# Weight quantisation in single steps, totals ahead of shares, and two input tiles moved, in a four-layer kernel

## The chip, the cores and the metric

The kernel runs on one core of one Trainium2 chip. A core has five engines that each work through their own queue of instructions in order: TensorE (PE in the profile, with its weight loads as PEld), VectorE (DVE), ScalarE (ACT), GpSimd (POOL) and SyncE (SP), which here issues DMAs. They wait for one another by semaphores. Matrix products are accumulated in PSUM banks of 128 partitions by 512 fp32 numbers; everything else lives in SBUF. The metric is the device time of one execution in microseconds (us), smaller is better.

## The reference

x has 2 sequences of 1024 tokens with 512 features. Four residual layers follow each other:

```python
x = x + attn_a(layernorm(x), w_in, w_out)                 # linear attention
x = x + ffn(layernorm(x), w_gate_up, w_proj)
x = x + attn_b(layernorm(x), Wq1, Wq2, Wk, Wv, Wlam, Wo)  # softmax attention
x = x + ffn(layernorm(x), w_gate_up, w_proj)              # same weights again
```

Linear attention projects to q, k, v, a and g. With k = tanh(k), a = clip(sigmoid(a + 2), 0.6, 0.9995) and u = k·v it runs a recurrence along the tokens, mem = a·mem + u, in chunks of 64, and returns (gate·(q·mem) + (1 − gate)·v) @ w_out.T, with q scaled by its root mean square per head and gate = sigmoid(g).

The feed-forward first makes its weights ternary: in groups of 64 numbers, scale = mean(|w|), and w becomes −scale, 0 or +scale, whichever of round(w / scale) it is. Then silu(x @ Wg)·(x @ Wu), an RMS norm, and the product with the ternary w_proj.

Attention b is differential: 16 heads, two sets of queries, causal softmax for each, and

```python
y = softmax(q1 k^T / sqrt(d)) v - sigmoid(x Wlam) * softmax(q2 k^T / sqrt(d)) v
```

followed by Wo.

## The kernel before

**Data.** The 2048 tokens lie in 16 residual tiles `xres` of 128 tokens by 512 features. A *block* is 512 tokens, four tiles; there are four blocks t. Features are handled in four *feature chunks* c of 128.

**Stage a, linear attention (14 to 390 us).** For each block, and in it for each feature chunk c: TensorE projects k and v (`kv`) and a and g (`ag`, both L315); ScalarE takes the tanh, the copy of v and the two sigmoids out of PSUM (L446 to L452); GpSimd multiplies u = k·v (L455) and later u·prefix (L466); VectorE clips a, makes the running product `prefix`, scales q (L471), and runs the recurrence as one scan (L477); then mem·q on VectorE (L482), mem − v on GpSimd (L483), mem·gate on VectorE (L484) and the addition of v to `yt` on GpSimd (L485). In the last step (t=3, c=3) the GpSimd work is given to VectorE. When all four `yt` are there, TensorE makes `a_out` (L509) and VectorE adds it to `xres` (L514).

Between these the next block's input is prepared. Its tiles are normalised on VectorE (L128: `xn_a`, one in c=0, one in c=1, two in c=2) and turned (transposed) by TensorE (L137) in c=2 and c=3. In the last block it is the first feed-forward block's input instead: `layernorm_begin` after c=0 (mean and variance on VectorE, L109/L110, and a square root on ScalarE), its reciprocal and four normalised tiles after c=1, the turns in c=3 (`xnt_f`).

**The weights on the side.** The feed-forward weights are quantised during stage a, in 16 *weight chunks* f, each of three tiles of 128 by 512 (class `Ternary`, L178). `begin` takes magnitude and sign on ScalarE, `mean` makes one matmul for each of the three tiles (`pm`, L203), whose result ScalarE casts to `scale`, and `finish` is six VectorE operations on 128x1536 numbers: the maximum with a floor (L208), the comparison `one` (L211), subtract, add, multiply (L213 to L215) and the product with the sign (L216). The result is stored to DRAM (`w_kept`) and the next chunk begins. `quantise(i)` (L361) calls `mean` for i = 0, 1, 2, and for i = 3 the whole finish. The lists `pieces` (L415 to L418) say which of these happen where in a step c.

**What sets the order.** In stage a the orders of TensorE and VectorE are those in which the code calls them (`manual_schedule`), and operations with no such place, the mean and variance of later blocks, are fitted in by a scheduler. The orders of ScalarE and GpSimd come from the scheduler. A tile pool that has no free buffer delays the operation that asks for one.

**Feed-forward 0 (395 to 764 us)** and **feed-forward 1 (1770 us to the end)** go block by block through the 16 weight chunks (L595 the gate and up products, L616 the down product). During one block the next block's input is made: its mean and variance (`layernorm_stats`), four normalised tiles, their turns, ScalarE's cast to `xs` and VectorE's `rest` (L165). The pool of the mean and variance is `norm`, with two buffers of each kind.

**Stage b, attention b (764 to 1770 us).** It goes through 32 pairs of heads, 16 to a sequence, each in `STEPS` = 6 steps. TensorE makes scores `s` (L872), whose maxima VectorE takes (L882, L887), then scores again transposed (`t`, L933, L941), ScalarE the exponential (L949), TensorE the weighted values `y` (L971). `weigh` copies a finished y to `ys` (L988) and sends it on by four DMAs from SyncE: for each of two heads its *share* of the output (L991) and the row of the softmax *totals* (L996, `tot`). When a sequence is done, `divide` (L1001) takes the reciprocal of the totals (48x512, L1004), multiplies the second set by lambda (L1006) and splits the factors in two (L1010, L1011); `combine` (L1013) spreads them by a matmul `r` (L1018), multiplies the shares (L1021) and subtracts them on GpSimd (L1022). `b_out` (L1035) follows. `at(n, step, ...)` hangs such work on a step of a pair. For sequence 0 it lies in the first pairs of sequence 1; for sequence 1 in a tail with its own fixed order on VectorE as well (L1158 to L1184), together with the turns of feed-forward 1's first input (`first_input`, L1047).

Of the kernel before, what the change touches and what calls it, by code (L numbers as in the profile page):

```python
# [14 lines left out]
ALU = mybir.AluOpType  # L15
# [27 lines left out]
def kernel(  # L43
# [59 lines left out]
    def layernorm_begin(tiles, name):  # L103
# [15 lines left out]
    def layernorm_stats(tiles, name):  # L119

        return layernorm_end(*layernorm_begin(tiles, name))
# [56 lines left out]
    class Ternary:  # L178
# [27 lines left out]
        def finish(self, dst):  # L206
            scale, mag = self.scale, self.mag
            nc.vector.tensor_scalar(scale, scale, SCALE_MIN, None, ALU.max)  # L208

            one = self.pool.tile(self.shape, BF, tag="one", name=f"one{self.n}", bufs=1)  # L210
            nc.vector.scalar_tensor_tensor(one, scale, TERNARY_CUT, mag, ALU.mult, ALU.is_lt)  # L211

            nc.vector.tensor_sub(scale, scale, mag)  # L213
            nc.vector.tensor_add(scale, scale, mag)
            nc.vector.tensor_mul(scale, scale, one)  # L215
            nc.vector.tensor_mul(dst, scale, self.sign)  # L216


    with ExitStack() as s:
# [141 lines left out]
        def quantise(i):  # L361

            now = chunk[0]
            if i < 3:
                now.mean(i, bank)
                return
            now.finish(now.w)
            nc.sync.dma_start(out=w_kept[now.f].bitcast(F32), in_=now.w.bitcast(F32))
            chunk.pop(0)
            if chunk:  # L370
                chunk[0].begin()
            if now.f + 3 < NF:
                chunk.append(Ternary(tp, now.f + 3, range(3)))
# [34 lines left out]
        for t in range(NBLK):  # L408
            yt = wa.tile([P, NKC, BLK], F32, tag="yt", name=f"yt{t}")
            last = t == NBLK - 1  # L410
            for c in range(NKC):
# [3 lines left out]
                if not last:  # L415
                    pieces = ((2,), (), (3,)) if c % 2 else ((0,), (1,), ())
                else:
                    pieces = (((0, 1), (2,), (3,)), ((0, 1), (2,), ()), ((), (), ()))[max(c - 1, 0)]  # L418
# [5 lines left out]
                if t + c == 0:  # L424
                    quantise(3)
                if not last and c > 1:
# [16 lines left out]
                if last and c == NKC - 1:  # L443
                    quantise(3)
# [29 lines left out]


# [7 lines left out]
                other.tensor_sub(mem, mem, v)  # L483
                nc.vector.tensor_mul(mem, mem, gate)  # L484
                other.tensor_add(yt[:, c, :], mem, v)  # L485
                if last and c == 0:
# [8 lines left out]
                for i in pieces[2]:  # L495
                    quantise(i)
# [9 lines left out]
            for j, k in products:  # L506
# [5 lines left out]
                if k == NKC - 1:  # L512
                    xi = xres[t * TPB + j]
                    nc.vector.tensor_add(xi, xi, po[j])  # L514
                    if not last:
# [4 lines left out]
                        for i in ((), (), (3, 0), (1, 2, 3))[j]:  # L520
                            quantise(i)
            if not last:
# [725 lines left out]
```

## Time and profile before

| | |
|---|---|
| median of three runs | 2144.16 us (2143.34 to 2144.2) |
| the profiled execution | 2142.4 us, its span 2140.7 us |
| mean granted TensorE clock | 0.994 |
| TensorE busy | 2106.4 us, 98% of the span |
| VectorE busy | 1077.7 us, 50% |
| ScalarE busy | 835.1 us, 39% |
| GpSimd busy | 445.0 us, 21% |

The profile is of one execution. Busy times do not add up to the span, since the engines work beside each other. The windows view splits it by stage; columns are the stretch in us, its length, busy time (and count) of TensorE, its weight loads, VectorE, ScalarE and GpSimd, the mean granted clock, the DMA share and GB/s:

```profile
14.00:104.00 90.00, 90.00 (x235) 42.06 (x234) 55.99 (x70) 38.95 (x56) 22.15 (x16) 1.00 0.34 129
104.00:180.00 76.00, 75.83 (x196) 34.71 (x194) 55.61 (x66) 34.68 (x47) 17.04 (x12) 1.00 0.23 83
180.00:262.00 82.00, 81.76 (x204) 36.85 (x204) 61.53 (x72) 37.13 (x49) 18.60 (x14) 1.00 0.18 67
262.00:390.00 128.00, 115.25 (x286) 52.28 (x285) 99.87 (x134) 47.52 (x68) 24.89 (x19) 0.95 0.22 82
1250.00:1270.00 20.00, 17.43 (x84) 8.23 (x85) 12.89 (x33) 4.64 (x13) 5.46 (x16) 0.83 0.03 8
1720.00:1770.00 50.00, 46.65 (x191) 21.40 (x192) 31.05 (x45) 12.61 (x28) 13.21 (x16) 1.00 0.33 119
```

In a timeline row the first number is the start in us from the beginning of the span, the second how long the instruction (or the group of equal ones, xN) took, then engine, line, operation, output and inputs; in brackets the idle time of the engine before it and what ended that.

### The profile page before, as it was taken

The numbers are of one execution on the slowest core, as the hardware profiler recorded it, in microseconds if no ns is written. First come the engines' busy times: TensorE is split into PE (matmuls) and PEld (weight loads), VectorE is DVE, ScalarE is ACT, GpSimd is POOL, SyncE is SP. The second block draws the span as 40 slices with busy tenths as digits, with TensorE's granted clock in tenths as the row PEclk, the third lists the DMA queues.
The fourth block names the chain that finished last, engine by engine and source line by source line (L and its number), as shares of the span: only waits on it lengthen the run. The fifth ranks groups of instructions, "written<-read, shape, count | busy, mean of one in ns | idle before, by whom it ended". The sixth has DMA issues, their size and how long they took to land.

```text
span 2140.7 us, 28058 instructions
## 1 busy us (share of the span) xinstructions
PE 2106.4 (98%) x10632; PEld 1245.6 (58%) x10632; DVE 1077.7 (50%) x2276; ACT 835.1 (39%) x1589; POOL 445.0 (21%) x808
## 2 busy tenths in 40 slices
PE   8999998899999999999999999999999999999998
PEld 4444444688888854444444444444444447888887
DVE  5676868433434235555555555464646662433332
ACT  5343543244334322444444422343434523333332
POOL 1312212121221221111111113021212221222212
PEclk9999999999999999999999999999999999999999
DMA  7121211600000111111110101201010033000000
GB/s 268 37 83 59 89 71 47 250 1 1 1 1 1 35 47 38 41 26 41 26 41 21 46 8 37 57 19 46 20 33 14 14 111 133 20 1 20 1 21 20
DMA packets 50999, 98.71 MB, mean 46 GB/s; under 512 B 10800, under 2 KB 19120, under 8 KB 50864
## 3 DMA queue, kind: packets, MB, share of 16 engines
q1 hardware_dynamic: 50864, 96.93, 13.8%
q8 instruction: 83, 1.36, 0.3%
q14 instruction: 52, 0.43, 0.1%
HBM read 58.75 MB, written 16.78 MB: 35 GB/s over the span
## 4 chain that ended last, share of the span: by engine, by line
PE 91%; DVE 5%; ACT 1%; issue 1%; POOL 1%; DMA 1%; SPq 0%; DVEq 0%; ACTq 0%; POOLq 0%
PE y L971 13%; PE g L595 11%; PE u L595 11%; PE f_out L616 11%; PE s L872 10%; PE pq L804 8%; PE t L933 8%; PE ag L315 4%; PE kv L315 4%; PE pv L769 3%; PE b_out L1035 2%; PE a_out L509 2%; PE mt L912 1%; PE t L941 1%; DVE one L211 1%
## 5 line engine op out<-in xcount | busy, mean ns | idle before, releaser
L949 ACT ACTIVATE pr<-t 128x512 f32<-128x512 f32 (+3 forms) x768 | 314.7, 497 | 383.5 <-PE t L941 383.3
L882 DVE CUSTOM_DVE_ANT_0 s<-s,causal 128x128 f32<-128x128 f32 (+3 forms) x512 | 245.3, 510 | 126.7 <-PE s L872 117.9
L971 PE MATMUL y<-pr,val 128*64 128x512 f32 (+3 forms) x1536 | 291.6, 501 | 1.3 <-ACT ys L988 1.3
L610 POOL TENSOR_TENSOR ssq<-ssq,sq 128x512 f32<-128x512 f32 x120 | 156.0, 1300 | 606.7 <-ACT sq L609 606.7
L601 DVE TENSOR_TENSOR h<-h,u 128x512 f32<-128x512 f32 x128 | 88.0, 688 | 360.6 <-PE u L595 354.5
L595 PE MATMUL g<-xs,w 128*128 128x512 f32 x1024 | 260.9, 397 | 0.0
L616 PE MATMUL f_out<-w,hs 128*128 128x512 f32 x1024 | 257.7, 394 | 0.3 <-DVE hs L604 0.3
L887 DVE TENSOR_REDUCE nmax<-s 128x1 f32<-128x512 f32 x256 | 164.9, 686 | 181.7 <-PE s L872 181.6
L595 PE MATMUL u<-xs,w 128*128 128x512 f32 x1024 | 256.3, 392 | 0.0
L872 PE MATMUL s<-gr,gr 32*128 32x512 f32 (+3 forms) x1536 | 249.8, 493 | 2.6 <-DVE nmax L882 2.6
L595 PEld LDWEIGHTS u<-xs,w 128*128 128x128 f32 x1024 | 192.2, 188 | 43.4
L616 PEld LDWEIGHTS f_out<-w,hs 128*128 128x128 f32 x1024 | 191.6, 188 | 43.9 <-DVE hs L604 1.1
L595 PEld LDWEIGHTS g<-xs,w 128*128 128x128 f32 x1024 | 190.1, 188 | 42.8 <-issue 1.0
L971 PEld LDWEIGHTS y<-pr,val 128*64 128x64 f32 x1536 | 93.7, 136 | 181.1 <-issue 105.7
L933 PE MATMUL t<-gr,gr 32*128 32x512 f32 (+3 forms) x1536 | 198.8, 533 | 0.0
L804 PE MATMUL pq<-b_xt,w_qk 128*128 128x512 f32 x384 | 176.1, 603 | 0.2 <-DVE x L633 0.2
L872 PEld LDWEIGHTS s<-gr,gr 32*128 32x128 f32 x1536 | 148.6, 186 | 46.7 <-issue 13.3
L603 ACT CAST hs<-h 128x512 fp32r<-128x512 f32 x128 | 79.4, 621 | 236.6 <-DVE h L601 236.6
L600 ACT ACTIVATE h<-g 128x512 f32<-128x512 f32 x128 | 76.6, 598 | 243.6 <-PE g L595 243.5
L952 POOL TENSOR_SCALAR_AFFINE_SELECT pr<-pr 128x256 f32<-128x256 f32 x256 | 101.5, 409 | 331.8 <-ACT pr L949 331.8
L604 DVE TENSOR_TENSOR hs<-h,hs 128x512 fp32r<-128x512 f32 x128 | 88.6, 692 | 83.1 <-ACT hs L603 83.1
L804 PEld LDWEIGHTS pq<-b_xt,w_qk 128*128 128x128 f32 x384 | 69.6, 189 | 88.4 <-issue 74.0
(160 smaller groups left out, 2218.9 us busy)
## 6 DMA issues: line engine op xcount, KB each, us to landing
w<-w_kept SPq DMA_DIRECT2D x32, 768.0 KB, 9.2
w_kept<-w SPq DMA_DIRECT2D x16, 768.0 KB, 3.2
gr<-gr SPq DMA_DIRECT2D x96, 128.0 KB, 2.3
w<-in_w_gu_dram SPq DMA_DIRECT2D x32, 256.0 KB, 2.9
share<-ys SPq DMA_DIRECT2D x128, 64.0 KB, 2.0
x<-in_x_dram SPq DMA_DIRECT2D x16, 256.0 KB, 6.1
w<-in_w_pt_dram SPq DMA_DIRECT2D x16, 256.0 KB, 3.6
w_qk<-in_wq_dram SPq DMA_DIRECT2D x8, 512.0 KB, 4.5
```

The costliest lines, as they stand in the source:

```text
L315: nc.tensor.matmul(po, w[:, k, ts(c, P)], xt[:, k, :], start=(k == 0), stop=(k == NKC - 1))
L595: nc.tensor.matmul(po, ws[f][:, part, ts(k, P)], xs[:, e, k, :], start=(k == 0 and e == 0), stop=(k == NKC - 1 and e == 1),)
L610: nc.gpsimd.tensor_add(ssq, ssq, sq)
L616: nc.tensor.matmul(po[j], hp[:, e, ts(j, P)], ws[f][:, 2, :], start=(f == 0 and e == 0), stop=(f == NF - 1 and e == 1),)
L804: nc.tensor.matmul(po, w[:, k, ts(kind, P)], xts[b][:, k, ts(e, BLK)], start=(k == 0), stop=(k == NKC - 1),)
L872: nc.tensor.matmul(part, queries[:, ts(j, P)], keys[:, first : first + nk], start=True, stop=True,)
L882: nc.vector.tensor_tensor_reduce(part, part, causal[:, BLK - part.shape[-1] :], -1.0, 3.0e38, ALU.add, ALU.min, top,)
L887: nc.vector.tensor_reduce(top, part, AX.X, ALU.max, negate=True)
L933: nc.tensor.matmul(banks[u, e][:, :nq], keys[:, ts(kb, P)], queries[:, (qb + 1) * BLK - nq : (qb + 1) * BLK], start=True, stop=False,)
L949: nc.scalar.activation(pr[:, e, :nq], banks[u, e][:, :nq], AF.Exp)
L952: nc.gpsimd.affine_select(out=pr[:, :, :P], in_=pr[:, :, :P], compare_op=ALU.is_ge, fill=0.0, base=0, pattern=[[0, 2], [1, P]], channel_mu ...
L971: nc.tensor.matmul(y[64 * e : 64 * e + 64, lo:], all_values[:, HV * (NH * kb + h) : HV * (NH * kb + h) + 64], pr[:, e, : BLK - lo], start= ...
```

## The change

1. `finish` becomes a generator of its six operations, and `quantise(3)` only puts them into a list `steps`. `step(1)` issues one, `step()` all that are left, then the store and the next chunk's `begin`. In the recurrence of a feature chunk, the floor is issued ahead of the scan, the comparison between mem·q and mem·gate, and the other four after mem·gate; the addition to `yt` is called before them.
2. Weight chunks are spread otherwise. Block 0 finishes six (one more: chunk 1 in c=0, 2 in c=1, 3 in c=3), the last block two, chunk 14 in c=0 and 15 in c=1 (before: chunk 13 behind c=0, 14 behind c=1, and 15 in c=3, behind the rests of the feed-forward's input). The three `pm` matmuls move with it. The next layer's `layernorm_begin` is called behind chunk 14's last steps.
3. The mean and variance of the later feed-forward blocks take their buffers from the stage's own pool `fp`, not from `norm`. As the instructions stand in order, those of blocks 1 and 2 of feed-forward 0 (eight pairs of operations) now lie inside the last recurrence, t=3, c=3, and the four of block 1 of feed-forward 1 in the tail of stage b. The square root of the first feed-forward block's variance stands on ScalarE between the two sigmoids of t=3, c=1.
4. `weigh` issues the two rows of totals ahead of the two shares.
5. The reciprocal of `divide` goes in four pieces of 48x128 for sequence 0, with score maxima between them.
6. The turns, casts and rests of the first two input tiles of feed-forward 1 go from the tail into steps 0 and 2 of the last pair, and the order of the tail is combine, turn 2, combine, turn 3, rest 2, rest 3.

```diff
--- before.py
+++ after.py
@@ -100,7 +100,7 @@
 
     norm = ctx.enter_context(tc.tile_pool(name="norm", bufs=2, reuse_waits="tile"))
 
-    def layernorm_begin(tiles, name):
+    def layernorm_begin(tiles, name, norm=norm):
 
         n = len(tiles)
         mv = norm.tile([P, n, 2], F32, tag="ln_mv", name=f"mv_{name}")
@@ -116,9 +116,9 @@
         nc.vector.reciprocal(rstd, rstd)
         return mv, rstd
 
-    def layernorm_stats(tiles, name):
-
-        return layernorm_end(*layernorm_begin(tiles, name))
+    def layernorm_stats(tiles, name, norm=norm):
+
+        return layernorm_end(*layernorm_begin(tiles, name, norm))
 
     def normal(i, j, stats, name, xn=None):
 
@@ -204,16 +204,18 @@
             nc.scalar.copy(self.scale[:, i, :], pm)
 
         def finish(self, dst):
+
             scale, mag = self.scale, self.mag
-            nc.vector.tensor_scalar(scale, scale, SCALE_MIN, None, ALU.max)
+            v = nc.vector
+            yield v.tensor_scalar(scale, scale, SCALE_MIN, None, ALU.max)
 
             one = self.pool.tile(self.shape, BF, tag="one", name=f"one{self.n}", bufs=1)
-            nc.vector.scalar_tensor_tensor(one, scale, TERNARY_CUT, mag, ALU.mult, ALU.is_lt)
-
-            nc.vector.tensor_sub(scale, scale, mag)
-            nc.vector.tensor_add(scale, scale, mag)
-            nc.vector.tensor_mul(scale, scale, one)
-            nc.vector.tensor_mul(dst, scale, self.sign)
+            yield v.scalar_tensor_tensor(one, scale, TERNARY_CUT, mag, ALU.mult, ALU.is_lt)
+
+            yield v.tensor_sub(scale, scale, mag)
+            yield v.tensor_add(scale, scale, mag)
+            yield v.tensor_mul(scale, scale, one)
+            yield v.tensor_mul(dst, scale, self.sign)
 
 
     with ExitStack() as s:
@@ -364,13 +366,24 @@
             if i < 3:
                 now.mean(i, bank)
                 return
-            now.finish(now.w)
-            nc.sync.dma_start(out=w_kept[now.f].bitcast(F32), in_=now.w.bitcast(F32))
-            chunk.pop(0)
-            if chunk:
-                chunk[0].begin()
-            if now.f + 3 < NF:
-                chunk.append(Ternary(tp, now.f + 3, range(3)))
+            steps.extend([now.finish(now.w)] * 6)
+            steps.append(now)
+
+        steps = []
+
+        def step(n=7):
+
+            for _ in range(min(n, len(steps) - 1) if n < 7 else len(steps)):
+                one = steps.pop(0)
+                if one is not chunk[0]:
+                    next(one)
+                    continue
+                nc.sync.dma_start(out=w_kept[one.f].bitcast(F32), in_=one.w.bitcast(F32))
+                chunk.pop(0)
+                if chunk:
+                    chunk[0].begin()
+                if one.f + 3 < NF:
+                    chunk.append(Ternary(tp, one.f + 3, range(3)))
 
         order = ExitStack()
         fixed = {mybir.EngineType.PE, mybir.EngineType.DVE}
@@ -414,8 +427,10 @@
 
                 if not last:
                     pieces = ((2,), (), (3,)) if c % 2 else ((0,), (1,), ())
+                    if t == 0 and c < 2:
+                        pieces = ((0, 1), (2,), (3,))
                 else:
-                    pieces = (((0, 1), (2,), (3,)), ((0, 1), (2,), ()), ((), (), ()))[max(c - 1, 0)]
+                    pieces = ((0, 1), (2,), (3,)) if c < 2 else ((), (), ())
                 project(kv[:, 0, :], w_k, c, xt)
                 if t + c == 0:
                     roots()
@@ -423,6 +438,7 @@
                 project(kv[:, 1, :], w_v, c, xt)
                 if t + c == 0:
                     quantise(3)
+                    step()
                 if not last and c > 1:
                     for j in (2 * c - 4, 2 * c - 3):
                         following.turn(j)
@@ -440,8 +456,8 @@
                 project(ag[:, 1, :], w_g, c, xt)
                 for i in pieces[1]:
                     quantise(i)
-                if last and c == NKC - 1:
-                    quantise(3)
+                for i in pieces[2]:
+                    quantise(i)
                 u = ap_.tile([P, BLK], F32, tag="u", name=f"u{n}")
                 nc.scalar.activation(u, kv[:, 0, :], AF.Tanh)
                 v = ap_.tile([P, BLK], F32, tag="v", name=f"v{n}")
@@ -472,6 +488,9 @@
                 if not last and c < 2:
                     following.normal(c)
 
+                if steps:
+                    step(1)
+
 
                 mem = ap_.tile([P, BLK], F32, tag="mem", name=f"mem{n}")
                 nc.vector.tensor_tensor_scan(
@@ -481,8 +500,11 @@
                 nc.vector.tensor_copy(before[c], mem[:, BLK - 1 : BLK])
                 nc.vector.tensor_mul(mem, mem, qn)
                 other.tensor_sub(mem, mem, v)
+                if steps:
+                    step(1)
                 nc.vector.tensor_mul(mem, mem, gate)
                 other.tensor_add(yt[:, c, :], mem, v)
+                step()
                 if last and c == 0:
                     ff_stats = layernorm_begin(range(TPB), "f0_0")
                 elif last and c == 1:
@@ -492,8 +514,6 @@
                     ff_first = FeedForwardInput(0, 0, edge_sb, "xt", ff_stats, room)
                     for j in range(TPB):
                         ff_first.normal(j)
-                for i in pieces[2]:
-                    quantise(i)
 
             if not last:
                 xt = following.xt
@@ -519,6 +539,7 @@
                             factors()
                         for i in ((), (), (3, 0), (1, 2, 3))[j]:
                             quantise(i)
+                            step()
             if not last:
                 q, rq = q_next, rq_next
                 following = Input(t + 2) if t + 2 < NBLK else None
@@ -669,7 +690,10 @@
                         if j == -2:
 
                             place = (edge_sb, "xt") if t % 2 else (xsp, "xs")
-                            following = FeedForwardInput(which, t + 1, *place)
+                            tiles = range((t + 1) * TPB, (t + 2) * TPB)
+
+                            measured = layernorm_stats(tiles, f"f{which}_{t + 1}", fp)
+                            following = FeedForwardInput(which, t + 1, *place, measured)
                         if j + 1 in range(TPB):
                             following.normal(j + 1)
                         if j >= 0:
@@ -986,22 +1010,27 @@
                     [P, NKC, SEQ], F32, tag=f"share{g // 2}", name=f"share{b}_{g // 2}"
                 )
             nc.scalar.copy(ys, y)
+
             for e in range(2):
-                i = 2 * p + e
-                nc.sync.dma_start(
-                    out=shares[b, g // 2][ts(i, HD), 2 * c + par, ts(qb, BLK)],
-                    in_=ys[64 * e : 64 * e + HD],
-                )
-                h = 8 * c + 2 * i + par
+                h = 8 * c + 2 * (2 * p + e) + par
                 nc.sync.dma_start(
                     out=totals[b][32 * (g // 2) + h : 32 * (g // 2) + h + 1, ts(qb, BLK)],
                     in_=ys[64 * e + HD : 64 * e + HV],
                 )
+            for e in range(2):
+                nc.sync.dma_start(
+                    out=shares[b, g // 2][ts(2 * p + e, HD), 2 * c + par, ts(qb, BLK)],
+                    in_=ys[64 * e : 64 * e + HD],
+                )
 
         def divide(b, e):
 
             part = totals[b][:, ts(e, BLK)]
-            nc.vector.reciprocal(part, part)
+
+            pieces = 1 if b else NKC
+            for i in range(pieces):
+                piece = part[:, ts(i, BLK // pieces)]
+                nc.vector.reciprocal(piece, piece)
             second = part[rows_of[1]]
             nc.vector.tensor_mul(second, second, lams[b][rows_of[1], ts(e, BLK)])
             factors[b, e] = b_c.tile([96 + NH, BLK], F32R, tag="factors", name=f"factors{b}_{e}")
@@ -1116,6 +1145,9 @@
         n = len(pairs) - 1
         at(n, 0, lambda: hold(("o", 1), load_out, 1))
         at(n, 0, lambda: hold("ff", first_input))
+
+        for j in range(2):
+            at(n, 2 * j, lambda j=j: held["ff"].tile(j, ring_bank))
         at(n, 3, divide, 1, 0)
 
 
@@ -1158,14 +1190,10 @@
         ordered.enter_context(tc.manual_schedule(engines={mybir.EngineType.DVE}))
         ff, w_o = held["ff"], held["o", 1]
 
-        ff.turn(0, ring_bank)
-        ff.turn(1, ring_bank)
         combine(1, 0, 0)
         ff.turn(2, ring_bank)
+        combine(1, 1, 0)
         ff.turn(3, ring_bank)
-        ff.rest(0)
-        ff.rest(1)
-        combine(1, 1, 0)
         ff.rest(2)
         ff.rest(3)
```

## The prediction

> **What bounds the kernel now.** I read the page first, then the waits of TensorE, then the time lines of every engine around each of its long waits.
>
> ```profile
> PE 2106.4 (98%) x10632; PEld 1245.6 (58%) x10632; DVE 1077.7 (50%) x2276; ACT 835.1 (39%) x1589; POOL 445.0 (21%) x808
> ```
> ```profile
> PE xnt_a L137 <- DVE xn_a L128: 7.6, 3, 6.0
> PE a_out L509 <- DVE q L471: 6.8, 1, 6.8
> PE xnt_f L137 <- DVE q L471: 5.6, 1, 5.6
> PE s L872 <- DVE nmax L882: 2.6, 1, 2.6
> PE y L971 <- ACT ys L988: 1.3, 2, 0.7
> PE b_out L1035 <- POOL share L1022: 1.2, 1, 1.2
> ```
>
> TensorE is never short of work except in these rows (waited for: total, times, longest). The 7.6 is the start and is not touched. The change can win three things: the two waits of the last linear-attention block (5.6, 6.8), the one where attention b goes from batch 0 to 1 (2.6), and the small ones before the second feed-forward.
>
> A long wait costs more than itself. TensorE around the first three (start, length, work, idle before it):
>
> ```profile
> 366.24 1.12 PE L137 MATMUL xnt_f<-ident,xn_f 128*128 128x128 f32 x4 [5.64 <-DVE q L471]
> 367.15 5.62 PE L315 MATMUL ag<-a_xt,w_in 128*128 128x512 f32 x8
> 384.98 10.48 PE L509 MATMUL a_out<-w_out,yt 128*128 128x512 f32 x20 [6.82 <-DVE q L471]
> 1252.57 2.46 PE L872 MATMUL s<-gr,gr 32*128 32x384 f32 x8 [2.60 <-DVE nmax L882]
> 1254.95 3.68 PE L971 MATMUL y<-pr,val 128*64 128x512 f32 x8
> 1260.57 1.73 PE L971 MATMUL y<-pr,val 128*64 128x512 f32 x8
> ```
>
> Eight matmuls behind the wait take 5.62 us where eight kv matmuls of the same form take 3.60 elsewhere (2.0 lost), and y takes 3.68 against 1.73 (with its neighbours about 3 lost). The granted clock reads 0.50 there. After idle of 0.6 to 1.2 us nothing of the kind follows. So a wait of 2.6 us or more costs itself plus 2 to 3 us. The Trainium skill ("TensorE: Matmul & The Clock Gate", Part 1: The HAM clock gate) gives the half clock only after an idle window of about 3.4 us; by that rule 1252.57 would run at full clock and be worth 2.60 alone; the trace has the half clock after 2.60 us, and the trace decides.
>
> **Block 0 of linear attention: the cost.** Weight chunk 1's six ternary finishing operations go from behind feature chunk c=1 into c=0, three of its mean matmuls with them (from the last block). The matmuls start 0.22 apart: 0.65 us on TensorE. The six operations meet GpSimd, which works between them. What such a meeting costs is in the old place (start, length):
>
> ```profile
> 62.18 1.18 DVE L128 TENSOR_SCALAR xn_a<-x,mv_a,rstd_a 128x512 f32<-128x512 f32 x1
> 67.56 1.51 POOL L485 TENSOR_TENSOR yt<-mem,v 128x512 f32<-128x512 f32 x1 [0.81 <-DVE mem L484]
> 67.99 2.70 DVE L211 SCALAR_TENSOR_TENSOR one<-scale,mag 128x1536 bf16<-128x1536 bf16 x1
> 69.04 2.78 POOL L455 TENSOR_TENSOR u<-u,v 128x512 f32<-128x512 f32 x1
> 65.49 1.04 PE L137 MATMUL xnt_a<-ident,xn_a 128*128 128x128 f32 x8
> ```
>
> The cut takes 2.70 instead of 1.76 when alone (row of 40.48), u 2.78 instead of 1.27: one waits the other out. The Trainium skill ("SBUF — State Buffer", Terms) calls the port pair that the two share lock-allocated, exclusive, held for the full instruction; by that rule interleaving gains nothing, and the rows agree.
>
> In c=0 I let the two engines take turns in order, with the rows' lengths: mem*q 53.6, cut 54.2–56.0, GpSimd's sub to 57.0, gate 57.7, sub 58.6, GpSimd's yt 59.6, add 60.4, u 61.4, mul 62.3, last mul 64.1. ScalarE's next magnitude waits for that add and its sign for the last mul (weight buffer free), 1.48 each; the sigmoid a of c=1 is behind them in its order: 65.6 instead of 58.59. DVE then needs the same 4.8 us as now from that sigmoid to the end of x̂ of the next block (row 62.18): 70.5 instead of 63.36. TensorE turns it from 65.49+0.43 (the other tile's turn)+0.65=66.57. Wait: 4 us, plus the half clock, 2 to 3: I take 4.0+2.5+0.65=**+7.1** (6.6 to 7.9; without any meeting, 1.0 of wait and no drop, +1.7). After it TensorE and DVE are both 7 us late, so the later turns keep their margin. In blocks 1 and 2 the chunk of c=1 keeps its place; only its scale and cut move ahead of the gate, where the cut delays GpSimd's sub by 1.6 and the queue is as long: 168.9 against 168.5 for its end. The tiles behind it are ready 2.9 us before their turn at 172.29. Cost 0.
>
> **Last block: the gain.** Here DVE is the bound: from 329.28 to q's end at 384.92 it stands idle for under 5 us. Three chunks become two: the finish behind c=2 (rows 373.62 to 380.65) goes, 7.0. Of the twelve mean-and-variance pairs that the scheduler has between 329 and 361 (0.66+0.17 each), eight are taken from a larger pool and now stand in c=3, five of them ahead of q: three leave the stretch, 2.5. Against that, both remaining chunks are now interleaved and meet GpSimd's sub, yt and u (the rows above: 0.94 to 1.5 a meeting): 1.5 to 3.3. Sum: 6.2 to 8.0 earlier, I take **−7.1**. Queues in detail: chunk 14's end 337.9, q of c=2 362.6 instead of 366.2 so the wait of 5.64 goes; a_out still waits about 5.5, since TensorE arrives earlier too. ScalarE's square root with its table load (1.28) now stands ahead of gate 3_1, done 343.3, when TensorE wants that bank at 340.8: a new wait of 2.5, a half clock too, but within the stretch that DVE sets: no term. If no meeting cost anything it would be −13.5. Chunk 15's mean matmuls are gone from here (0.65), hidden by the wait.
>
> **Batch 0 to 1 of attention b: the gain.**
>
> ```profile
> 1245.03 0.59 SPq L996 DMA_DIRECT2D tot<-ys  x1
> 1246.30 0.59 SPq L996 DMA_DIRECT2D tot<-ys  x1
> 1248.02 3.35 DVE L1004 RECIPROCAL tot<-tot 48x512 f32<-48x512 f32 x1 [1.00 <-DMA tot<-ys]
> ```
>
> Totals issued ahead of shares: the second leaves the queue at about 1245.03 instead of 1246.30, lands 1.25 earlier. That is 64 swaps; shares are read much later, so the others are free. The reciprocal goes in four pieces with score work between, each 3.35/4 plus a fixed part of about 0.1 (a 128x1 row takes 0.13 to 0.18): 0.94, 0.4 more in all. The scores that TensorE waits 2.60 for then come after one or two pieces: about 0.3+0.6+1.1 of waits in place of one of 2.60. None reaches the lengths that halved the clock, so 2.6−2.0 plus 2 to 3 would be 2.7 to 3.1; if the clock falls nonetheless, 0 to 0.6. I give the first 7 in 10 and take **−2.0**.
>
> **Into the second feed-forward.**
>
> ```profile
> 1720.51 1.72 PE L971 MATMUL y<-pr,val 128*64 128x512 f32 x8 [0.69 <-ACT ys L988]
> 1726.19 1.94 PE L971 MATMUL y<-pr,val 128*64 128x512 f32 x8 [0.58 <-ACT ys L988]
> 1730.96 3.35 DVE L1004 RECIPROCAL tot<-tot 48x512 f32<-48x512 f32 x1 [11.43 <-DMA tot<-ys]
> 1736.25 0.73 PE L1018 MATMUL r<-factors,head_of 112*128 112x512 f32 x2 [0.91 <-DVE factors L1011]
> ```
>
> The last total was issued at 1729.11 behind a slow share and will leave at about 1726.7: reciprocal 2.4 earlier, r up to 2.0 earlier. Two tiles' turns (0.5 each) move up into the two waits of 0.69 and 0.58. The wait of b_out for GpSimd's share (1.2) stays. DVE gets four mean-and-variance pairs (3.3) here, partly ahead of the second factors. Second b_out 1753.46 → about 1751.9: **−1.5** (−0.3 to −2.1). The moved casts and subtractions lie beside TensorE's scores; ScalarE (39%) and DVE (50%) cover them.
>
> **Sum.** 7.1−7.1−2.0−1.5=−3.5. The profiled execution took 2142.4 (span 2140.7), 1.8 below the median of 2144.16; applied to that median: **2140.7**. From no change I could tell 0.2%, 4.3 us.
>
> **Rivals.**
> *Meetings are cheap.* If DVE and GpSimd mostly miss each other, block 0 costs 1.7 to 4 and the last block yields 10 to 13.5: about −10, **2134**. For: an order of several engines shifts by fractions of a us, and one us less lateness in block 0 also brings its wait near the lengths that keep the clock. Against: the meeting rows above, one for each chunk of the old kernel.
> *A second wait of this kind* (the other side). The turn in c=3 of blocks 0, 1 and 2 has about 2.9 us left. If the interleaved chunk in c=1 ends more than 2.9 later than worked out (three meetings more), each block waits 2 and pays the half clock, 4.5; with two or three of them +9 to +13.5 on the sum: +5.5 to +10, **2151**. Against: the number of meetings in c=1 is the same as before.
> *The clock falls in attention b as before, and the pairs lengthen the tail*: 0 and −0.3 in place of −2.0 and −1.5: −0.3, **2143.9**.
>
> **How the numbers follow.** Forecast 0.42 (own range 2137.5 to 2143.5), cheap meetings 0.27, second wait 0.15, nothing in attention b 0.16. The forecast's case reaches below 2139.9 in about two fifths. Faster 0.27+0.17=0.44; same 0.24+0.14=0.38; slower 0.15 and a little of the last: 0.18. The range leaves out the far ends of the two outer cases: 2132 to 2149.
>
> **What would show it.** Right: a wait of xnt_a on x̂ of about 4 us near 66.6 with the clock at 0.5 behind it; no wait of xnt_f in the last block; a_out's wait still above 4; the first matmul g of the feed-forward within 1.5 us of 394.89; three short waits in place of 2.60 near 1250; r near 1734. Wrong: block 0 without that wait, or q of c=3 before 375 (cheap meetings); waits of xnt_a near 172 (second wait); y above 3 us behind 1250.

## The result, and the profile after

The changed kernel takes 2138.96 us (median of 20 runs, 2137.29 to 2141.72), the kernel before 2143.29 beside it (20 runs, 2140.95 to 2144.99): a ratio of 0.9982, with a 95% interval of 0.9976 to 0.9988. That is 4.3 us less, where the prediction had 3.5 less. The size came out right, by luck: two parts that the prediction did not have, of about 10 us each and of opposite signs, cancel.

The waits of TensorE after (waited for: total, times, longest). In stage a `pq` is the query product, `sq` its square on ScalarE, and `pss` the matmul that averages the squares for q's scale; `pv` in attention b is the product for its values:

```profile
PE xnt_a L137 <- DVE xn_a L128: 11.5, 4, 6.1
PE pss L329 <- ACT sq L339: 7.0, 3, 2.4
PE ag L317 <- ACT gate L468: 2.9, 2, 2.8
PE a_out L529 <- DVE q L487: 2.6, 1, 2.6
PE b_out L1064 <- POOL share L1051: 1.2, 1, 1.2
PE s L896 <- DVE nmax L906: 0.9, 2, 0.5
```

The wait of xnt_f (5.6) is gone, a_out's fell from 6.8 to 2.6, s's from 2.6 to 0.9. New are 3.9 of xnt_a, 2.8 of ag and 7.0 of pss. Here are the same matmuls in both profiled executions; the last column is what the stretch that ends there brought.

| start of | before | after | difference | of this stretch |
|---|---|---|---|---|
| first query product after block 0 (pq) | 88.94 | 95.98 | +7.04 | +7.0 |
| last group of a_out of block 2 | 300.85 | 318.01 | +17.16 | +10.1 |
| first g of feed-forward 0 | 394.89 | 403.08 | +8.19 | −9.0 |
| first pq of attention b | 762.30 | 765.75 | +3.45 | −4.7 |
| first pv of sequence 1 | 1265.15 | 1268.70 | +3.55 | +0.1 |
| first g of feed-forward 1 | 1770.33 | 1773.11 | +2.78 | −0.8 |
| end of the span | 2140.7 | 2138.4 | −2.3 | −5.1 |

**Block 0.** The timeline after, VectorE and GpSimd in c=0, ScalarE behind them, then TensorE:

```profile
54.78 1.75 DVE L213 SCALAR_TENSOR_TENSOR one<-scale,mag 128x1536 bf16<-128x1536 bf16 x1
59.28 1.91 DVE L216 TENSOR_TENSOR scale<-scale,mag 128x1536 bf16<-128x1536 bf16 x1
54.94 2.71 POOL L502 TENSOR_TENSOR mem<-mem,v 128x512 f32<-128x512 f32 x1 [2.87 <-DVE mem L501]
65.03 1.48 ACT L195 ACTIVATE sign<-w 128x1536 bf16<-128x1536 f32 x1 [2.27 <-DVE w L218]
66.42 0.67 ACT L466 ACTIVATE a<-ag,two 128x512 f32<-128x512 f32 x1
71.22 0.66 PE L137 MATMUL xnt_a<-ident,xn_a 128*128 128x128 f32 x4 [3.94 <-DVE xn_a L128]
```

GpSimd's subtraction takes 2.71 beside the cut instead of 1.27, VectorE's add 1.91 instead of 0.96. The sign waits for the last product of the weight chunk (`w`), the sigmoid stands behind the sign, and TensorE waits 3.94.

**The ends of blocks 0, 1 and 2.** ScalarE at the end of block 1, first before, then after, with TensorE's row:

```profile
194.46 1.48 ACT L193 ACTIVATE mag<-w 128x1536 bf16<-128x1536 f32 x1 [5.05 <-DVE scale L214]
195.85 0.57 ACT L335 COPY q<-pq 128x512 f32<-128x512 f32 x1
196.32 0.60 ACT L337 ACTIVATE sq<-pq 128x512 f32<-128x512 f32 x1
197.25 1.48 ACT L195 ACTIVATE sign<-w 128x1536 bf16<-128x1536 f32 x1 [0.33 <-DVE w L216]
```
```profile
203.00 1.48 ACT L193 ACTIVATE mag<-w 128x1536 bf16<-128x1536 f32 x1 [4.40 <-DVE scale L216]
205.79 1.48 ACT L195 ACTIVATE sign<-w 128x1536 bf16<-128x1536 f32 x1 [1.31 <-DVE w L218]
207.18 0.57 ACT L337 COPY q<-pq 128x512 f32<-128x512 f32 x1
207.65 0.60 ACT L339 ACTIVATE sq<-pq 128x512 f32<-128x512 f32 x1
208.30 2.08 PE L329 MATMUL pss<-sq,headmean 128*128 128x512 f32 x2 [2.38 <-ACT sq L339]
```

Before, q's copy and square stood between the next chunk's magnitude and its sign. After, the sign is ahead of them, and ScalarE waits 1.31 for the chunk's last product before it can start it. The chunk itself ends no later: the sign starts 16.1 us behind the first pq of this group, against 16.8 before (189.66 and 180.47). It is the order that is late. TensorE's order is fixed, and it waits 2.38. Behind two of the three such waits the clock is halved (pss takes 2.08 instead of 1.13 for two).

**Last block and attention b**, TensorE after:

```profile
360.88 8.83 PE L317 MATMUL ag<-a_xt,w_in 128*128 128x512 f32 x16 [2.76 <-ACT gate L468]
394.20 5.42 PE L529 MATMUL a_out<-w_out,yt 128*128 128x512 f32 x12 [2.61 <-DVE q L487]
1254.46 1.13 PE L896 MATMUL s<-gr,gr 32*128 32x384 f32 x4 [0.45 <-DVE nmax L906]
1256.03 1.93 PE L896 MATMUL s<-gr,gr 32*128 32x384 f32 x4 [0.44 <-DVE nmax L906]
1257.88 3.68 PE L995 MATMUL y<-pr,val 128*64 128x512 f32 x8
```

The reciprocal is in pieces and starts 1 us earlier against its neighbours, and two waits of 0.45 stand for the one of 2.60. But y still takes 3.68 for eight: the clock fell all the same. The windows view, by the us (after the length: busy time and count of TensorE, weight loads, VectorE, ScalarE, GpSimd; then the granted clock):

```profile
1254.00:1255.00 1.00, 0.55 (x3) 0.40 (x3) 1.00 (x6) 0.75 (x2) 0.15 (x1) 1.00 0.00 0
1255.00:1256.00 1.00, 0.59 (x4) 0.26 (x2) 0.98 (x3) 0.00 (x0) 0.72 (x4) 1.00 0.00 0
1256.00:1257.00 1.00, 0.97 (x2) 0.67 (x3) 0.96 (x2) 0.00 (x0) 0.98 (x2) 0.61 0.00 0
1257.00:1258.00 1.00, 1.00 (x5) 0.46 (x6) 0.96 (x2) 0.00 (x0) 0.65 (x2) 0.50 0.00 0
```

Whether the clock falls is not settled by the length of a wait. The same two waits in a later run (e6 below, with the same code in the last block) are as long as here:

```profile
353.11 7.13 PE L317 MATMUL ag<-a_xt,w_in 128*128 128x512 f32 x16 [2.77 <-ACT gate L468]
386.45 10.50 PE L530 MATMUL a_out<-w_out,yt 128*128 128x512 f32 x20 [2.61 <-DVE q L487]
```

Behind the gate's wait the sixteen ag take 7.13 there and 8.83 here; behind q's wait the last twenty a_out take 9.9 us to the first g there and 8.9 here. One wait halves the clock in the one execution and the other in the other. In all fourteen profiles a stretch at half clock lasts 3.41, 6.83, 10.24 or 13.65 us, one to four times 3.41 (apart from the one that the end of the trace cuts off), and within an execution all changes of the clock lie on one grid of 3.41 us. So where a wait falls on that grid counts as well, and a single profile can be off by 1 to 2 us for each such wait.

**The feed-forwards.** The groups of instructions in four stretches (busy us, mean ns of one): before, in block 0 (405 to 480 us) and block 1 (500 to 570), then after in the same two:

```profile
L595 PE MATMUL u<-xs,w 128*128 128x512 f32 x104 | 26.4, 395 | 0.0
L616 PE MATMUL f_out<-w,hs 128*128 128x512 f32 x104 | 26.2, 394 | 0.0
...
L616 PE MATMUL f_out<-w,hs 128*128 128x512 f32 x104 | 26.0, 392 | 0.0
L595 PE MATMUL u<-xs,w 128*128 128x512 f32 x98 | 24.3, 389 | 0.0
```
```profile
L616 PE MATMUL u<-xs,w 128*128 128x512 f32 x112 | 27.7, 389 | 0.0
L637 PE MATMUL f_out<-w,hs 128*128 128x512 f32 x104 | 25.7, 389 | 0.0
...
L637 PE MATMUL f_out<-w,hs 128*128 128x512 f32 x104 | 25.7, 389 | 0.0
L616 PE MATMUL u<-xs,w 128*128 128x512 f32 x101 | 25.0, 389 | 0.0
```

Before, u takes 395 ns in blocks 0 and 2 and 389 to 390 in 1 and 3, and f_out 392 to 394 in blocks 0 to 2. After, both take 389 to 390 there. The g products, which come ahead of u, take 395 to 399 before and 394 to 395 after in these blocks; in block 3 f_out has a mean of 402 in both kernels. No matmul of these loops was changed, and TensorE hardly waits in them (0.4 us in all for hs). What did change is memory: the mean and variance got buffers in the feed-forward's pool, 192 bytes per partition, and what is allocated behind that pool moved up by as much. The traces hold no addresses; the allocation gives these starts, modulo 256 bytes:

| | weights w | input xs, blocks 0 and 2 | input xs, blocks 1 and 3 | hs |
|---|---|---|---|---|
| before | 64 | 0 | 64 | 0 |
| after | 0 | 0 | 0 | 0 |

The slow pairs (u in blocks 0 and 2; f_out) are those whose two operands start at different places modulo 256. This is so far a reading of two kernels; e1, e2 and e8 below test it.

### The profile page after: what moved, and what is told of

Same layout as the page of the kernel before. It is cut to its first block, busy times and chain, and to the rows that moved or that the text cites. A ratio compares the mean times of both kernels' runs of the same rounds, so it can differ in the third digit from the quotient of the medians.

```text
span 2138.4 us, 28060 instructions
## 1 busy us (share of the span) xinstructions
PE 2103.5 (98%) x10632; PEld 1245.7 (58%) x10632; DVE 1083.6 (51%) x2282; ACT 834.9 (39%) x1589; POOL 462.3 (22%) x808
## 4 chain that ended last, share of the span: by engine, by line
PE 89%; DVE 7%; ACT 2%; POOL 1%; DMA 1%; issue 1%; SPq 0%; DVEq 0%; ACTq 0%; POOLq 0%
PE y L995 13%; PE g L616 11%; PE u L616 11%; PE f_out L637 11%; PE s L896 10%; PE pq L828 8%; PE t L957 8%; PE ag L317 3%; PE kv L317 3%; PE pv L793 3%; PE b_out L1064 2%; PE a_out L529 2%; PE mt L936 1%; POOL mem L502 1%; PE t L965 1%
```

## The experiments

Every run is set beside runs of the kernel before on the same chip (2142.85 to 2143.73). The theory after the comparison: (1) the place of the weights makes the feed-forwards quicker; (2) the interleaving costs the waits of pss; (3) the moved chunk costs block 0 what it gains in the last block.

**e1: only the place of the weights, in the kernel before.**

```diff
                 inv = fp.tile([P, TPB], F32, tag="inv", name=f"inv{which}_{t}")
+                if t == 0:
+                    pad = fp.tile([P, 48], F32, tag="pad", name=f"pad{which}", bufs=1)
+                    nc.gpsimd.memset(pad, 0.0)
```

> The kernel before, with one unused tile of 192 bytes per partition added to the feed-forward's own pool: as in the changed kernel, the resident weights and the second input buffer then start 192 bytes later (a multiple of 256 bytes). Theory (place of the operands in memory): u and f_out matmuls go from 395 and 394 ns to 389 in all blocks, each feed-forward stage takes 4.5 to 5.3 us less, the whole 9 to 10 less, about 2133.5. Rival (the feed-forwards are quicker by chance of the execution, or because the mean and variance were moved): rows of 394 and 395 stay, time within 2 of the kernel before. Nothing else moves: the waits of 6.8, 5.6 and 2.6 stay.

Measured: 2132.13, ratio 0.9953 (0.9938 to 0.9968). The waits for q and nmax stayed (6.6, 5.6 and 2.6, against 6.8, 5.6 and 2.6). In feed-forward 0, between 500 and 570 us:

```profile
L595 PE MATMUL u<-xs,w 128*128 128x512 f32 x100 | 24.8, 390 | 0.0
L616 PE MATMUL f_out<-w,hs 128*128 128x512 f32 x98 | 24.3, 390 | 0.0
```

An unused tile in the kernel before wins more than twice what the whole change wins.

**e2: the place undone, in the changed kernel.** The same lines with 16 numbers instead of 48 (64 bytes).

> The changed kernel with an unused tile of 64 bytes per partition in the feed-forward's pool, so that the weights start 64 bytes off a multiple of 256 again, as in the kernel before, while mean and variance stay where the change puts them. Theory of place: u and f_out return to 394 and 395 in part of the blocks, +9 to +10, about 2148.8, slower than the kernel before. Rival (the moved mean and variance make the feed-forward quicker): 2139, as the change.

Measured: 2149.65, ratio 1.0032 (1.002 to 1.0044); u in block 0 at 396 again, f_out at 394, while the mean and variance are where the change puts them. It is the place, and without it the change would make the kernel slower.

**e3: steps together again, new distribution.**

```diff
-                if steps:
-                    step(1)
...
-                if steps:
-                    step(1)
```

> The changed kernel with the six finishing operations together again behind each step, in the new distribution. Theory: the three waits of pss for sq (2.3 each, with a half clock behind two of them) come from the interleaving, which puts the next chunk's sign ahead of the third sq on ScalarE; they fall to about 0.2, which gives back 9 to 10 in blocks 0 to 2. The wait in block 0 comes from the distribution and stays at 4 to 5. The last block may lose 0 to 2. About 2131. Rival (the interleaving makes block 0's wait, not the chunk's move): block 0's wait goes below 1.5, and the time to 2125. Rival (the pss waits come from the later place of the chunk, whatever its order): pss stays at 2.3, time 2139.

Measured: 2131.19, ratio 0.9947 (0.9932 to 0.9962). The waits of pss fell to 0.8 in three, and block 0's wait stayed (xnt_a 11.3 in four, the first ones of the start among them). Both as the theory had it. ScalarE's order at the end of block 1 is the old one again (copy at 202.41, square at 202.87, sign at 203.80). No run keeps the single steps and only moves the sign behind the square.

**e4: old distribution, interleaved steps.**

```diff
-                    if t == 0 and c < 2:
-                        pieces = ((0, 1), (2,), (3,))
...
-                    pieces = ((0, 1), (2,), (3,)) if c < 2 else ((), (), ())
+                    pieces = (((0, 1), (2,), (3,)), ((0, 1), (2,), ()), ((), (), ()))[max(c - 1, 0)]
...
+                if last and c == NKC - 1:
+                    quantise(3)
+                    step()
```

> The changed kernel with the old distribution of weight chunks (five in block 0, three in the last block) and the interleaved steps. Theory: block 0's wait of 3.9 and its half clock go (stage a 7 less up to the end of block 0), the waits of pss stay at about 2.3, the last block gets back a wait of xnt_f and a longer one of a_out, 8 to 10 more. About 2141. Rival (the interleaving makes block 0's wait): a wait of 3 or more of xnt_a near 66 stays, 2147.

Measured: 2141.34, ratio 0.9994 (0.9984 to 1.0004). Block 0's wait is gone (xnt_a 6.8 in three), pss still waits 7.0, a_out 10.4. The expected wait of xnt_f did not come back; ag waits 3.0 for the gate instead.

**e9: both undone, old distribution and steps together.** The edits of the last two.

> The changed kernel with both parts that concern the weight chunks undone: the old distribution, and the six finishing operations together. What is left of the change is the moved mean and variance (with the place of the weights), totals ahead of shares, the reciprocal in pieces and the two input tiles. Against the kernel before with 192 bytes of padding (2132.1): the tail gives 0.75, attention b's turn to sequence 1 0 to 1.5, and block 0 and the waits of pss are as before. About 2130.7. Rival (the mean and variance that now lie in the last recurrence lengthen it): a_out's wait goes from 6.6 to 9 or more, 2134.

Measured: 2132.25, ratio 0.9951 (0.9938 to 0.9965): the same as the kernel before with padding (2132.13). So all the rest of the change (totals first, pieces, input tiles, moved mean and variance) comes to nothing together, apart from the place of the weights. The rival has a part in it: a_out waits 10.5, and the first g starts at 396.66 against 395.19 with padding alone, which takes back the tail's 0.8. The four combinations:

| | steps together | interleaved |
|---|---|---|
| old distribution | 2132.25 | 2141.34 |
| new distribution | 2131.19 | 2138.96 |

The runs are of different chips, but the ratios to the kernel before say much the same: interleaving costs 8 to 9, and the distribution gives 1 to 2. All four have the weights on a multiple of 256, which e1 and e2 price at 10.7 each.

**e5: is block 0 held by that one tile?**

```diff
                 if not last and c < 2:
-                    following.normal(c)
+                    for j in (c,) if t else ((0, 1), ())[c]:
+                        following.normal(j)
```

> The changed kernel; block 1's second input tile is normalised in block 0's c=0 already, beside the first, ahead of weight chunk 1's steps, where it was in c=1. Theory: TensorE's wait of 3.94 for it and the half clock behind (2.5) are the whole cost of block 0's extra chunk, and go; a wait of under 1 for gate 0_1 takes their place. End of block 0 6 earlier, about 2133. Rival (TensorE is held in block 0 by the late recurrence itself, the tile is only the first to show): another wait of 3 or more in c=2 or c=3 of block 0, time 2137 to 2139.

Measured: 2140.05 (2135.76 to 2143.67), ratio 0.9985 (0.9976 to 0.9994). My theory fell. The rival expected one wait of 3 or more; instead the wait of 3.94 went, and these came, in c=2 and c=3:

```profile
69.43 0.38 PE L203 MATMUL pm<-mag,groupmean 128*128 128x512 bf16 x1 [0.38 <-ACT scale L204]
85.85 1.06 PE L137 MATMUL xnt_a<-ident,xn_a 128*128 128x128 f32 x8 [1.47 <-DVE xn_a L128]
87.93 0.58 PE L203 MATMUL pm<-mag,groupmean 128*128 128x512 bf16 x1 [1.02 <-ACT scale L204]
88.43 8.50 PE L317 MATMUL ag<-a_xt,w_in 128*128 128x512 f32 x16
```

They add up to 2.9, and ag takes 8.50 instead of 7.03 behind them. From the first turn of a tile to the first pq it is 29.0 us against 29.3 in the changed kernel, and 23.5 before. My reading, which no run isolates, is that VectorE and ScalarE have two chunks in a row to finish there, and the lateness only shows at another tile.

**e6: steps together in blocks 0 to 2, interleaved in the last.** The early tiles of e5, and `if steps and last:` at both places.

> As the run before this one, and the steps of a chunk are interleaved in the last block only; in blocks 0 to 2 they stand together behind the recurrence's step. The theories add up: against the changed kernel the waits of pss (10 with their half clocks) and block 0's wait (6) both go, the last block keeps its interleaving (worth 1 to 1.5 against all six together). About 2123. Rival (what is taken from one wait comes back in the last block, where VectorE is the bound): 2127 or more.

Measured: 2130.16, ratio 0.994 (0.9927 to 0.9954), close to the 2131.19 of e3. The gains did not add up to the 2123 expected: block 0 still costs (the first pq starts at 96.19), and the interleaving in the last block is worth 1 or nothing.

**e7: does the place matter in attention b?** On top of e6:

```diff
-        b_a, b_p, b_b, b_c, b_d = (
+        b_a, b_p, b_b, b_c, b_d, b_e = (
...
-        all_values = b_d.tile([P, NQ * NH * HV + 64 - HV], F32, name="val")
+        all_values = b_e.tile([P, NQ * NH * HV + 64 - HV], F32, name="val")
```

with `nmax` and `rest` in `b_e` as well.

> As the run before this one; in attention b the small tiles of maxima and the values are moved into a pool of their own behind the others, so that every operand of its matmuls starts on a multiple of 256 bytes; before, they start 0, 64 or 192 beyond one. Theory of place, if it holds for these matmuls too: pq (3.48 for eight against 3.43 of the projections in stage a) and the scores of every second pair become 1 to 2% shorter, 3 to 8 in all, 2115 to 2120. Rival (it holds only for the feed-forward's operands): no difference from the run before this one within 1.

Measured: 2132.28 (2130.65 to 2132.73) against 2130.16 (2129.62 to 2132.51). The medians are 2.1 apart, more than the rival's 1, but nothing became faster; s stays at 492 ns, t at 533, pq at 603. The rival holds: the plain fp32 matmuls here do not care.

**e8: how far apart?** The padding of 64 bytes in the kernel before.

> The kernel before with 64 bytes of padding in the feed-forward's pool: its weights start 128 bytes beyond a multiple of 256, the first input buffer on one. If the distance between the two operands counts modulo 128: u and f_out at 389 to 390, as with 192 bytes, 2133.5. If modulo 256: 393 to 395 in blocks 0 and 2, 2143.

Measured, in one execution: 2143.73; u 395 in blocks 0 and 2 and 390 in block 1 (where both operands start at 128), f_out 395. A distance of 128 bytes is as slow as one of 64, and operands that start alike are as quick at 128 as at 0 (after) and 64 (before, block 1): the distance counts, not the place of either. Counted from their place in the kernel before, the weights lie 0, 64 and 256 bytes on in the slow kernels (before, e8, e2) and 192 in the quick ones (after, e1), which is why it is counted modulo 256; no run has a distance of 192.

**e10: the gate's wait in the last block.** On top of e6:

```diff
-                step()
                 if last and c == 0:
                     ff_stats = layernorm_begin(range(TPB), "f0_0")
-                elif last and c == 1:
+                step()
+                if last and c == 1:
```

> The run with plain steps until the last block and both tiles early (2130.2); in the last block the mean and variance of the feed-forward's first input are taken ahead of chunk 14's steps, so that ScalarE has the square root done before it needs gate 3_1. Prediction's theory (VectorE sets the end of the block, the gate's wait of 2.8 and its half clock lie within): that wait goes, a_out's grows from 2.6 by about 4, time within 1.5 of 2130.2. Rival (TensorE is by now the bound of that block too): 3 to 4.5 less, 2126 to 2127.

Measured: 2128.62, ratio 0.9934 (0.9921 to 0.9946). The wait of 2.8 went, xnt_f's grew from 0.46 to 1.86, a_out's stayed at 2.6, and the first g starts at 394.72 instead of 396.38. Neither theory: about 1.6 of the gate's wait was on the path, the rest was covered (in e6 no half clock follows it).

**e11: the reciprocal whole.** On top of e6, `pieces = 1`.

> The run with plain steps until the last block and both tiles early (2130.2); the reciprocal of sequence 0 in one piece again, the totals still ahead of the shares. If one short wait keeps the clock where several in 4 us do not: one wait of 1.3 to 1.6 of s for nmax near 1247 and y after it at 1.7 to 2.0 for eight, 1 to 1.5 less than that run, about 2129. Rival (the clock gate goes by how busy TensorE was over some us, not by the longest wait): y after it still at 3.3 to 3.7, no difference within 1.

Measured: 2130.85, ratio 0.9938 (0.9926 to 0.9951). TensorE in that run:

```profile
1247.72 2.66 PE L897 MATMUL s<-gr,gr 32*128 32x512 f32 x10 [1.66 <-DVE nmax L907]
1250.30 3.18 PE L996 MATMUL y<-pr,val 128*64 128x512 f32 x8
```

One wait of 1.66, and the clock falls as it does behind two of 0.45 (y at 3.20 in e6). No gain from the pieces shows; the totals ahead of the shares have shortened the wait from 2.60. The profile is of one execution: two of this run's five took 2128.05 and 2128.22 with a mean clock of 0.998, the others 2130.85 to 2131.76 with 0.996.

**e12: mean and variance into the feed-forward.** On top of e10, the working tile comes from a ring that is in use until then:

```diff
+                            room = fp.tile([P, BLK], F32, tag="sq", name=f"st_f{which}_{t + 1}")
-                            measured = layernorm_stats(tiles, f"f{which}_{t + 1}", fp)
+                            measured = layernorm_stats(tiles, f"f{which}_{t + 1}", fp, room)
```

where `layernorm_begin` takes `st = room[:, 8 * j : 8 * j + 6]`, and 64 bytes of padding keep the weights in place.

> As e10_variance_ahead_of_chunk (2128.6); the mean and variance of the later feed-forward blocks take their working tile from the feed-forward's ring of squares, so that they come in the middle of the block before, and none of their pairs lies in the last recurrence or in the tail of attention b (the weights still start on a multiple of 256 bytes). If the five pairs ahead of q (0.83 each, 4.2) are on the path that ends stage a: a_out's wait of 2.6 goes, the first g comes 2.6 to 4 earlier, the tail 0 to 1, about 2125.5. Rival (they lie in VectorE's idle time): no difference within 1 of 2128.6.

Measured: 2125.79 (2125.28 to 2126.34), ratio 0.9917 (0.9904 to 0.9931). a_out no longer waits for q:

```profile
376.17 14.15 PE L533 MATMUL a_out<-w_out,yt 128*128 128x512 f32 x32 [0.20 <-POOL yt L510]
389.76 2.41 PE L620 MATMUL g<-xs,w 128*128 128x512 f32 x8
```

The first g is 5.0 earlier than in e10's profile, in which the half clock follows a_out's wait; the medians differ by 2.8. This version beats both kernels, by 17.9 and 13.2 us.

## Why the prediction came out right, and where it was wrong

**Block 0, +7.1: right in size.** The wait was 3.94 against 4.0, the stretch +7.0 (of which 0.5 is a later start of the execution). Taking turns between VectorE and GpSimd with the lengths of the rows gave the last product's end as 64.1; it was 64.93 in a run that started 0.5 later. The Trainium skill ("SBUF — State Buffer", Terms) has the loser at the shared port wait for the whole instruction; 2.71 against 1.27 and 1.91 against 0.96 agree. What was wrong is the reading of the wait as that of one tile (e5).

**"Cost 0" in blocks 1 and 2: wrong, by 10.1.** This step failed. I looked at the turns of the tiles behind the chunk of c=1, and these kept their margin as the prediction said: no xnt_a waits there. I did not follow the chunk of c=3, nor ScalarE's order behind it: the next chunk's sign ahead of the third query's copy and square. Each wait of pss is 2.3 to 2.4, in all three blocks, with half clocks behind two. e3 and e4 put it on the interleaving. The rival of a second wait had about this size (9 to 13.5), but at the turn in c=3, which never waited.

**Last block, −7.1: right in sign, 9.0 in size.** The wait of xnt_f went and the gate's came (2.76 against 2.5). Measured from the last group of a_out of block 2, a_out goes on behind q's wait 7.9 earlier than before, near the 7.1; the other 1.0 is the half clock, which did not follow a_out's wait in this execution and does in e6. That wait is 2.6 where I had 5.5, since TensorE itself came later, held by the gate. "No term" for the gate's wait was too little by about 1.6 (e10), and the mean and variance ahead of q were on the path as the sum had it (e12).

**Attention b, −2.0: wrong, +0.1.** The waits became short as predicted. The step that failed is that "none reaches the lengths that halved the clock": the clock does not go by one length. It fell behind 0.45+0.44 with TensorE 55 to 59% busy for two us, and behind a single 1.66 (e11), yet not behind a_out's 2.61. The rival with the clock falling as before is what came true here. The Trainium skill ("TensorE: Matmul & The Clock Gate", Part 1) ties the fall to an idle window of about 3.4 us. In attention b no wait is longer than 2.60 and the clock falls, so the measurement differs. From the last eight y ahead of these waits to the first pv it is 19.0 us before and 19.1 after, both with 6.83 us at half clock. It is 17.6 in e3 and e6, whose code is the same here, with 3.41 us: the 1.5 between them is the clock's, not the change's. In e8, which has the old code and 3.41 us, it is 17.9.

**Tail, −1.5: −0.8.** r and the first b_out came 1.5 earlier against their neighbours; the second b_out only 0.8. The mean and variance on VectorE ahead of the second factors took the rest, e12's tail being 0.7 shorter without them.

**The feed-forwards, no term at all: −9.8.** I took the moved buffers for a matter of order alone. That a tile's address could change the length of a matmul was not among my rivals, and no wait shows it. The sum of what I priced would have been a loss: without the place of the weights, e2, the changed kernel is 0.32% slower than before. The range held because two misses of 10 us cancelled, which was luck. The prediction's own signs said so: the first g came at 403.08 and not within 1.5 us of 394.89, a_out's wait was under 4, and y stayed above 3 behind 1250.

## What to carry to other kernels

When a change adds, drops or moves a small tile, compare the lengths of untouched matmuls before and after, not only the waits: here 192 bytes were worth 10 us, and starting the operands of the long fp32r matmuls at the same place modulo 256 costs no more than such padding. Work that is cut into steps must be followed on every engine that is released by it; a finer order on VectorE cost 8 to 9 us because ScalarE's queue then put a late instruction ahead of a needed one. Where a wait goes, look for the queue that was late: taking away the wait of 3.9 us for one tile brought 2.9 us at three other places. And before a us or two at half clock is put down to a change, look at the same stretch in several profiles.

## What the runs showed of the hardware that I had not expected

- The u and f_out matmuls (fp32r, 128x512) whose two operands start 64 or 128 bytes apart modulo 256 take 392 to 396 ns in the profile, those that start alike 389 to 390 (blocks 0 to 2). Eight of them follow each other in 1.85 to 1.87 us instead of 1.81 to 1.82. Over two feed-forwards that is 10.7 us (e1, e2). The weight loads take 188 ns either way. Why is open; attention b's fp32 matmuls show nothing of the kind (e7).
- The clock was halved behind two waits of 0.45 us with TensorE busy in between, and behind one of 1.66; it was not behind one of 2.61 (after) and one of 2.77 (e6). It changes on a grid of 3.41 us in every execution, and that grid lies differently against the kernel's start in each.
